# Scatters of the first phase spread over slots, two weight chunks kept on chip, ids moved behind the stream: a macaron block on one core

## The chip, the core and the metric

The kernel runs on one core of a Trainium2 chip. Its engines are TensorE (PE for matmuls, PEld for loading the stationary operand), VectorE (DVE), ScalarE (ACT), GpSimd (POOL) and SyncE (SP), which here issues most DMAs. The metric is the device time of one execution in microseconds, lower is better.

## The reference, cut to what matters

```
x = x + 0.5 * ffn(layernorm(x))
x = x + attention(layernorm(x))          # groups of 64 tokens, 16 heads of 16, causal
x = x + 0.5 * ffn(layernorm(x))

def ffn(x):                              # 4096 tokens, H = 256
    xn = rmsnorm(x)
    p, i = top_k(softmax(xn @ router_w.T), 2)       # 8 experts
    rw = p / sum(p)
    # each expert takes its first 640 tokens, in order
    xg = x[dispatch]
    eout = (silu(xg @ rg) * (xg @ ru)) @ rd         # 256 -> 1024 -> 256, one for each expert
    routed = scatter_add(eout * weight)
    shared = silu(x @ sg) * (x @ su) @ sd           # 256 -> 2048 -> 256
    return shared + routed
```

Both feed-forward networks have the same weights and the same input layout. Results are float32.

## The kernel before

**Numbers.** Each float32 operand of a matmul is split into two float16 parts, hi and lo (`split`, L102 to L107: ACT makes hi on L105, DVE makes lo on L106). A product is three matmuls: hi by hi, hi by lo, lo by hi (`TERMS`).

**Phases.** There are 4096 tokens, in 32 tiles of 128 rows or 8 blocks of 512. Phase a runs the shared network of the first FFN over blocks 0 to 3 (`shared`, L392 on, 16 chunks of 128 columns for each block). Phase b runs the eight experts of the first FFN (`experts`, L435 on, 8 chunks each). Phase c runs the shared network for the other four blocks and then that of the second FFN for blocks 0 to 6. Phase d runs the second FFN's experts and its last shared block.

**The main stream.** A chunk of `shared` is 12 matmuls of 128x512 on L349 (gate and up) and 12 of 128x256 on L373 (down), 3.9 us together. Between them ACT makes sl on L360 (L356 in phases c and d), DVE multiplies it with up on L362, ACT rounds it to hh on L364, DVE takes the rest hl on L365. The down product of a chunk is deferred by one chunk, so that PE has the next gate product to run meanwhile. PSUM holds three gate and up tiles.

**The side stream.** Beside the main stream, `Tiles` (L696) runs one generator for each tile: load, layernorm statistics (`stats`, L142 to L150, whose last step rstd is a power on POOL), z on DVE (L162), split into X (`two`, L166), transposing DMA, router logits. A tile starts every `GAP_A` = 2 slots in phase a. A slot is run by `drive` (L739) after every 2.5 yields of the main stream, some 3.26 us. In phase c the side stream is the attention with the layernorm of the second FFN.

**Routing.** After the fourth tile of a block, `route` finds each token's two experts and their rows; a chain of small operations on POOL (L243 to L264) makes the weights. `scatter` (L322 to L337) then writes a tile's rows, with four tag columns behind them, to the experts' lists in DRAM: four copies (L328) and two indirect DMAs (L330), all on POOL. The block's four scatters come in four slots after one another; they stand behind `self.anchor` where that is set, and phase a does not set it.

**Expert rows.** `expert_load` (L416 on) loads an expert's tags (L420, SP) and its rows by a transposing DMA (L422, SP), and makes ids and weights of the rows on DVE (L429 to L433). `experts` loads a chunk's three weight pieces re (L446 twice and L449, SP), splits them into wc and wd, and runs the chunk for 640 rows. Two such buffers of each are there. Expert 0's rows are loaded at the end of phase a (and of c), while the main stream of that phase is still running.

**Order.** Each engine runs its instructions in one order, fixed when the kernel is built, by a scheduler that knows priorities and estimated times. `behind(True, k)` (L198) puts what is inside it behind the main stream's latest sl: k = 0 is ACT's on L360, k = 1 DVE's on L362. SP, POOL and each engine wait in that order: an instruction that waits for data holds those behind it.

Of the kernel before, what the change touches and what calls it, by code (L numbers as in the profile page):

```python
# [8 lines left out]
F32 = mybir.dt.float32  # L9
F32R = mybir.dt.float32r  # L10
F16 = mybir.dt.float16
BF16 = mybir.dt.bfloat16
I32 = mybir.dt.int32
# [7 lines left out]
P = 128  # L21
H = 256
# [15 lines left out]
class Net:  # L38
# [100 lines left out]
                self.split(self.sdw[:, 0, c:c + 2], self.sdw[:, 1, c:c + 2], r2)  # L139
            yield  # L140

    def stats(self, x, mv, rstd):  # L142
        nc = self.nc
        st = self.sm.tile([P, 6], F32, name="st")
        nc.vector.bn_stats(out=st, in_=x)
        nc.vector.bn_aggr(out=mv, in_=st)
        ve = self.sm.tile([P, 1], F32, name="ve")
        nc.vector.tensor_scalar(
            out=ve, in0=mv[:, 1:2], scalar1=LN_EPS, scalar2=1.0 / UP ** 2, op0=ALU.add, op1=ALU.mult)
        nc.gpsimd.tensor_tensor(out=rstd, in0=ve, in1=self.mhalf[:, :1], op=ALU.pow)  # L150

    def normed(self, x, mv, rstd, pool=False):

# [80 lines left out]
            fb["L"] = self.sm.tile([P, 4, 2, E], F32, name="L")  # L234
        nc.scalar.copy(fb["L"][:, t], p)

    def route(self, R, b, fb):

        nc = self.nc
        sm = self.sm  # L240
# [58 lines left out]
        if b == NB - 1:  # L299
            self.limits(R)  # L300
            yield
        for t in range(4):
            with self.tc.issue_after(self.anchor.ins) if self.anchor else nullcontext():
                self.scatter(R, b, fb, t, di, w1, dl, ef)
            yield

    def limits(self, R):

# [107 lines left out]
    def expert_load(self, R, e, hold):  # L416
        nc = self.nc
        rows = R["xg"][e * CAP:(e + 1) * CAP]
        tag = self.sm.tile([P, 5, 4], F32, name="tag")
        nc.sync.dma_start(out=tag, in_=rows[:, H:XW].rearrange("(t p) f -> p t f", p=P))  # L420
        xt = hold["x"] = self.xe.tile([P, 4, CAP], F16, name="xe")
        nc.sync.dma_start_transpose(out=xt, in_=rows[:, 0:H].bitcast(F16))  # L422
        yield
        yield
        yield
        ids = hold["id"] = self.cst.tile([P, 5], I32, name=f"eid{R['key']}{e}")
        w = hold["w"] = self.cst.tile([P, 5], F32, name=f"ew{R['key']}{e}")
        tk = self.sm.tile([P, 5], I32, name="tkb")
        nc.vector.tensor_tensor(out=tk, in0=tag[:, :, 0].bitcast(I32), in1=R["bits"][:, e], op=ALU.bitwise_and)  # L429
        nc.vector.tensor_tensor(out=ids, in0=tk.bitcast(F32), in1=R["off"][:, e], op=ALU.add)  # L430
        nc.vector.scalar_tensor_tensor(
            out=w, in0=tag[:, :, 3], scalar=float(e), in1=tag[:, :, 1], op0=ALU.is_equal, op1=ALU.mult)
        nc.vector.tensor_tensor(out=w, in0=w, in1=tag[:, :, 2], op=ALU.add)  # L433

    def experts(self, R, rg, ru, rd, cur, also=iter(())):  # L435

        nc = self.nc
        for e in range(E):
            x, ids, wts = cur["x"], cur["id"], cur["w"]
            outs = [self.ps_out.tile([P, BT], F32, name="po", tag="po") for _ in range(3)]  # L440
            cur = {}
            nxt = self.expert_load(R, e + 1, cur) if e < E - 1 else iter(())
            for c in range(8):
                r = self.raw.tile([P, 2, 2, P], F32, name="re", tag="raw")
                for i, s in enumerate((rg, ru)):
                    nc.sync.dma_start(  # L446
                        out=r[:, i], in_=s[e, :, c * P:(c + 1) * P].rearrange("(k p) f -> p k f", p=P))
                r2 = self.raw.tile([P, H], F32, name="re2", tag="raw2")
                nc.sync.dma_start(out=r2, in_=rd[e, c * P:(c + 1) * P])  # L449
                wc = self.raw.tile([P, 2, 2, 2, P], F16, name="wc")  # L450
                self.split(wc[:, 0], wc[:, 1], r)
                wd = self.raw.tile([P, 2, H], F16, name="wd")
                self.split(wd[:, 0], wd[:, 1], r2)
                h = self.hbuf()
                for t0, n in SUBS:
                    hs = [a[:, t0:t0 + n] for a in h]
                    for _ in self.gate_up(wc, x[:, :, t0:t0 + n], hs):
                        pass

                def fin(e=e, c=c, h=h, wd=wd, outs=outs, ids=ids, wts=wts):  # L460
                    self.down(outs, 5, h, wd, c, 8)
                    if c < 7:
                        return
                    key = R["key"], e
                    for t in range(5):
                        eo = self.raw.tile([P, H], F32, name="eo", bufs=5)
                        o = outs[t // 2][:, (t % 2) * H:(t % 2 + 1) * H]
                        if t % 2:
                            nc.scalar.activation(eo, o, AF.Copy, scale=wts[:, t:t + 1])
                        else:  # L470
                            nc.vector.tensor_scalar_mul(eo, o, wts[:, t:t + 1])  # L471
                        i = nc.gpsimd.indirect_dma_start(  # L472
                            out=R["acc"][:, :], out_offset=bass.IndirectOffsetOnAxis(ap=ids[:, t:t + 1], axis=0),
                            in_=eo, in_offset=None, bounds_check=T - 1, oob_is_err=False, compute_op=ALU.add).ins
                        if 0 < t < 4:
                            self.tc.declare_no_dep(i, group=str(key), reason="an expert's tokens are distinct")
                        self.tc.add_to_no_dep_group(str(key), i)

                self.defer(fin)
                next(nxt, None)  # L480
                if e and c in (2, 4, 6):
                    next(also, None)
            for _ in nxt:
                pass
# [177 lines left out]

    def front_steps(self, y, t, new_fb, keep=None):
        fb = new_fb(t)
        self.stats(y, fb["mv"][:, t, :], fb["rstd"][:, t:t + 1])
        yield
        X = self.xs.tile([P, XW], F32, name="X")
        xp = X[:, 0:H].bitcast(F16)
# [27 lines left out]
class Tiles:  # L696


    def __init__(self, make, count, gap, held=None):
        self.make, self.count, self.gap = make, count, gap  # L700
        self.held = held
        self.slot = 0
        self.live = []
        self.nxt = 0

    def done(self):
        return self.nxt == self.count and not self.live

    def steps(self):

# [3 lines left out]
        for one in list(self.live):  # L714
            with self.held.behind(one[0] >= 4 * PEB, 0, 1) if self.held else nullcontext():
                r = next(one[1], "end")
            if r == "end":
                self.live.remove(one)
            elif r == "stall":
                return  # L720
            yield
        self.slot += 1

# [35 lines left out]
def macaron(ctx, tc, x, w_qkv, ln_w, w_proj, router_w, rg, ru, rd, sg, su, sd, out):  # L759
# [20 lines left out]

    def tail(R, h, b, t):
        if t == 3:
            yield from n.route(R, b, fbs[(h, b)])

    def tile1(j):
        b, t = divmod(j, 4)
# [4 lines left out]
            nc.sync.dma_start(out=R1["acc"][j * P:(j + 1) * P], in_=y)  # L791
        yield from n.front_steps(y, t, new_fb(1, b))
        yield from tail(R1, 1, b, t)
        if j == 31:
            yield from n.expert_load(R1, 0, first[0])

# [14 lines left out]
    with n.phase("a", BT, 2, 16):  # L811
# [4 lines left out]
        n.keep_going(20)  # L816
        n.load_router(router_w)
        n.keep_going(16)
        tiles = Tiles(tile1, 32, GAP_A, n)
        run_slots(tiles, ready(1, 0))  # L820
        next(weights)
        for b in range(NA):
# [5 lines left out]
        n.experts(R1, rg, ru, rd, first[0], n.attn_weights(w_qkv, w_proj))  # L828
    with n.phase("c", BT, 2, 6, SLC):
        n.attn_init(ln_w)  # L830
        tiles = Tiles(tile2, 32, GAP_C)
        for b in range(NA, NB):
            drive(all_shared((1, b), b, R1["acc"], R1["acc"], tanh=True), tiles, RATE_C)
        for b in range(NC):
# [48 lines left out]
```

## Time and profile before

| what | us |
|---|---|
| median of 3 runs | 1821.59 (1820.73 to 1824.99) |
| the profiled execution | 1819.05 |
| its span in the profile | 1817.3 |
| PE busy | 1780.0 |
| DVE busy | 1194.9 |
| ACT busy | 951.5 |
| POOL busy | 753.0 |
| mean granted clock of PE | 0.996 of full speed |

The span is the profiled execution less 1.75 us around it. Busy times are those of instructions that compute or move, so a PE busy for 1780.0 us has 37 us in which no matmul ran, and some of the busy time is matmuls at a lower granted clock. In a row of a timeline the bracket gives the idle time of that engine ahead of the instruction and the instruction that ended it. A list of waits gives the same idle time, summed by what waited for what: total us, number, longest.

### The profile page before, as it was taken

To read this page: it belongs to the slowest core of one execution; us is meant where nothing else is said; L and a number is where in the kernel's file an instruction comes from. 1 tells how busy PE (TensorE), PEld (TensorE's weight loads), DVE (VectorE), ACT (ScalarE), POOL (GpSimd) and SP (SyncE) were. 2 spreads that over 40 slices of the span, in tenths; PEclk is the share of its full clock that TensorE was granted. 3 is DMA by queue.
4 is the path that set the end of the run, shared out by engine and by line. 5 is a ranking of instruction groups with operands and counts; after the bars stand their busy time and mean duration, and the time that the engine had idled before them with its cause. 6 is when DMAs were issued, how large, how long until landed. Compare 5 with 4: busy or idle time off the path is not lost.

```text
span 1817.3 us, 37386 instructions
## 1 busy us (share of the span) xinstructions
PE 1780.0 (98%) x13652; PEld 1199.6 (66%) x13652; DVE 1194.9 (66%) x2909; ACT 951.5 (52%) x2057; POOL 753.0 (41%) x1072
## 2 busy tenths in 40 slices
PE   8999999999999999999999999999999999999998
PEld 5655657777777556665656666566655677777765
DVE  6756546666666567877787777777756566666643
ACT  4433325555555456666666666666323455555542
POOL 6576620222111335576767677776430011122210
PEclk9999999999999999999999999999999999999999
DMA  7333142555453255667666675756212144455420
GB/s 215 89 105 112 41 69 73 129 127 118 112 118 75 59 102 96 133 115 140 123 134 135 117 152 111 143 101 127 59 28 66 35 108 110 115 116 124 98 48 13
DMA packets 439481, 185.95 MB, mean 102 GB/s; under 512 B 302337, under 2 KB 436669, under 8 KB 439296
## 3 DMA queue, kind: packets, MB, share of 16 engines
q1 hardware_dynamic: 420816, 161.60, 40.6%
q0 software_dynamic: 17664, 21.17, 6.9%
q8 instruction: 107, 1.75, 0.4%
q10 hardware_dynamic: 816, 0.79, 0.1%
q14 instruction: 78, 0.64, 0.1%
HBM read 78.95 MB, written 42.21 MB: 67 GB/s over the span
## 4 chain that ended last, share of the span: by engine, by line
PE 67%; POOL 9%; DVE 9%; issue 6%; ACT 5%; DMA 3%; SPq 1%; POOLq 0%; DVEq 0%; ACTq 0%
PE pgu L349 43%; PE po L373 21%; POOL xg L330 3%; DVE hl L365 2%; DVE sl L357 1%; DVE sl L362 1%; POOL S L607 1%; DVE amx L606 1%; ACT V L611 1%; ACT sl L356 1%; POOL rstd L150 1%; POOL X L328 1%; DVE S L601 1%; POOL e L618 1%; PE pqk L660 1%
## 5 line engine op out<-in xcount | busy, mean ns | idle before, releaser
L349 PE MATMUL pgu<-xb,sgu 128*128 128x512 f16 x3072 | 737.8, 380 | 8.9 <-DVE sl L357 5.6
L364 ACT CAST hh<-sl 128x512 f16<-128x512 f32 (+2 forms) x512 | 272.9, 533 | 535.9 <-DVE sl L362 533.3
L349 PE MATMUL pgu<-xe,wc 128*128 128x384 f16 (+1 forms) x3072 | 497.0, 299 | 0.0
L349 PEld LDWEIGHTS <-sgu 128*128 128x128 f16 x3072 | 293.1, 98 | 283.2 <-issue 15.8
L362 DVE SCALAR_TENSOR_TENSOR sl<-pgu,sl 128x512 f32<-128x512 f32 (+2 forms) x512 | 300.8, 588 | 244.9 <-PE pgu L349 218.1
L365 DVE TENSOR_TENSOR hl<-sl,hh 128x512 f16<-128x512 f32 (+2 forms) x512 | 316.0, 618 | 148.5 <-ACT hh L364 147.4
L373 PEld LDWEIGHTS <-hh 128*128 128x128 f16 x3328 | 321.2, 98 | 108.5 <-ACT hh L364 4.3
L349 PEld LDWEIGHTS <-wc 128*128 128x128 f16 x3072 | 300.6, 98 | 91.9
L373 PE MATMUL po<-sdw,hh 128*128 128x256 f16 x2048 | 349.6, 272 | 4.3 <-DVE xr L406 2.1
L373 PE MATMUL po<-sdw,hl 128*128 128x256 f16 x1024 | 249.4, 273 | 13.9 <-DVE hl L365 11.3
L373 PE MATMUL po<-wd,hh 128*128 128x256 f16 x1280 | 221.3, 273 | 0.0
L472 POOL DMA_INDIRECT out_dram<-eo,eidscatter x40 | 64.5, 1612 | 344.5 <-DVE eo L471 309.7
L373 PEld LDWEIGHTS <-hl 128*128 128x128 f16 x1664 | 162.7, 98 | 56.4 <-DVE hl L365 22.7
L360 ACT ACTIVATE sl<-pgu 128x384 f32<-128x384 f32 (+1 forms) x336 | 158.8, 473 | 62.5 <-PE pgu L349 34.4
L472 POOL DMA_INDIRECT acc<-eo,eidscatter x40 | 65.5, 1638 | 294.4 <-DVE eo L471 260.5
L357 DVE SCALAR_TENSOR_TENSOR sl<-sl,pgu 128x512 f32<-128x512 f32 x176 | 120.0, 682 | 53.9 <-ACT sl L356 52.8
L330 POOL DMA_INDIRECT xg<-X,di x128 | 132.1, 1032 | 50.0 <-issue 27.8
L373 PE MATMUL po<-wd,hl 128*128 128x256 f16 x640 | 147.9, 273 | 0.0
L105 ACT ACTIVATE wc<-re 128x512 f16<-128x512 f32 x128 | 80.6, 630 | 79.6 <-PE pgu L349 63.0
L356 ACT ACTIVATE sl<-pgu 128x512 f32<-128x512 f32 x176 | 104.3, 592 | 28.2 <-PE pgu L349 26.6
L106 DVE SCALAR_TENSOR_TENSOR wc<-re,wc 128x512 f16<-128x512 f32 x128 | 88.3, 690 | 28.8 <-ACT wc L105 28.6
L607 POOL TENSOR_TENSOR S<-S,amx 128x1024 f32<-128x1024 f32 x32 | 63.6, 1989 | 70.9 <-DVE amx L606 70.5
(155 smaller groups left out, 1725.2 us busy)
## 6 DMA issues: line engine op xcount, KB each, us to landing
re<-in_L_ffn_rg_dram SPq DMA_DIRECT2D x128, 128.0 KB, 2.4
re<-in_L_ffn_ru_dram SPq DMA_DIRECT2D x128, 128.0 KB, 2.4
re<-in_L_ffn_rd_dram SPq DMA_DIRECT2D x128, 128.0 KB, 2.5
y<-acc SPq DMA_DIRECT2D x64, 128.0 KB, 2.2
y<-in_L_attn_x_dram SPq DMA_DIRECT2D x32, 128.0 KB, 2.1
acc<-xr SPq DMA_DIRECT2D x16, 256.0 KB, 2.4
out_dram<-xr SPq DMA_DIRECT2D x16, 256.0 KB, 2.8
x<-y SPq DMA_DIRECT2D x28, 128.0 KB, 3.0
```

The source lines that it names most:

```text
L106: nc.vector.scalar_tensor_tensor(out=lo, in0=src, scalar=WS, in1=hi, op0=ALU.mult, op1=ALU.subtract)
L330: i = nc.gpsimd.indirect_dma_start(out=R["xg"][:, :], out_offset=bass.IndirectOffsetOnAxis(ap=di[:, t, k:k + 1], axis=0), in_=X, in_offset ...
L349: nc.tensor.matmul(p, lhsT=wc[:, w, i, k, :], rhs=x[:, 2 * a + k, :], start=(j == 0), stop=(j == 5))
L356: nc.scalar.activation(s, p, AF.Tanh, scale=0.5 / XP)
L357: nc.vector.scalar_tensor_tensor(out=s, in0=s, scalar=1.0, in1=p, op0=ALU.add, op1=ALU.mult)
L360: self.latest[0] = nc.scalar.activation(s, p, AF.Silu, scale=1.0 / XP).ins
L362: self.latest[1] = nc.vector.scalar_tensor_tensor(out=s, in0=ps[1], scalar=1.0 / XP / (2.0 * XP if tanh else 1.0), in1=s, op0=ALU.mult, op ...
L364: nc.scalar.copy(h[0], s)
L365: nc.vector.tensor_tensor(out=h[1], in0=s, in1=h[0], op=ALU.subtract)
L373: nc.tensor.matmul(o, lhsT=h[a][:, t * P:(t + 1) * P], rhs=wd[:, w], start=(c == 0 and j == 0 and t % 2 == 0), stop=(c == nch - 1 and j == 2),
L472: i = nc.gpsimd.indirect_dma_start(out=R["acc"][:, :], out_offset=bass.IndirectOffsetOnAxis(ap=ids[:, t:t + 1], axis=0), in_=eo, in_offset ...
L607: self.anchor = nc.gpsimd.tensor_tensor(out=S, in0=S, in1=mx.unsqueeze(2).to_broadcast([P, 16, 64]), op=ALU.subtract)
```

## The change

1. In phase a, the scatters of a block no longer run in the routing's own slots. They go to a list `tiles.extra`, from which one tile's scatter (four copies, two DMAs) is issued every two slots, behind the latest rstd on POOL, which `stats` now records as the anchor. The last block still has one tile for each slot, and phase c (`apart` = 1) too.
2. `first_chunks` loads the weights of the first expert's first two chunks in phase a (three DMAs of 256 KB), splits them there, and keeps the results in the constants' pool for both passes over the experts. Both passes then load expert 0's weights from chunk 2 on.
3. The four operations that make an expert's ids and weights are put behind the main stream's latest sl on DVE.

In the order of SP's instructions, where the experts begin, before had tag, rows (expert 0), the weights of chunk 0, tag, rows (expert 1), the weights of chunk 1; the changed kernel has tag, rows, tag, rows, the weights of chunk 2, of chunk 3. Before had the tags of six further experts in a row some places later; they are now one for each expert.

```diff
@@ -139,7 +139,7 @@
                 self.split(self.sdw[:, 0, c:c + 2], self.sdw[:, 1, c:c + 2], r2)
             yield
 
-    def stats(self, x, mv, rstd):
+    def stats(self, x, mv, rstd, anchor=False):
         nc = self.nc
         st = self.sm.tile([P, 6], F32, name="st")
         nc.vector.bn_stats(out=st, in_=x)
@@ -147,7 +147,9 @@
         ve = self.sm.tile([P, 1], F32, name="ve")
         nc.vector.tensor_scalar(
             out=ve, in0=mv[:, 1:2], scalar1=LN_EPS, scalar2=1.0 / UP ** 2, op0=ALU.add, op1=ALU.mult)
-        nc.gpsimd.tensor_tensor(out=rstd, in0=ve, in1=self.mhalf[:, :1], op=ALU.pow)
+        i = nc.gpsimd.tensor_tensor(out=rstd, in0=ve, in1=self.mhalf[:, :1], op=ALU.pow)
+        if anchor:
+            self.anchor = i
 
     def normed(self, x, mv, rstd, pool=False):
 
@@ -234,7 +236,7 @@
             fb["L"] = self.sm.tile([P, 4, 2, E], F32, name="L")
         nc.scalar.copy(fb["L"][:, t], p)
 
-    def route(self, R, b, fb):
+    def route(self, R, b, fb, tiles):
 
         nc = self.nc
         sm = self.sm
@@ -299,10 +301,19 @@
         if b == NB - 1:
             self.limits(R)
             yield
+        last = self.scatters(R, b, fb, di, w1, dl, ef, 1 if b == NB - 1 else tiles.apart)
+        if b == NB - 1 or tiles.apart == 1:
+            yield from last
+        else:
+            tiles.extra.append(last)
+
+    def scatters(self, R, b, fb, di, w1, dl, ef, every):
+
         for t in range(4):
-            with self.tc.issue_after(self.anchor.ins) if self.anchor else nullcontext():
+            with self.tc.issue_after(self.anchor.ins):
                 self.scatter(R, b, fb, t, di, w1, dl, ef)
-            yield
+            for _ in range(every):
+                yield
 
     def limits(self, R):
 
@@ -426,11 +437,31 @@
         ids = hold["id"] = self.cst.tile([P, 5], I32, name=f"eid{R['key']}{e}")
         w = hold["w"] = self.cst.tile([P, 5], F32, name=f"ew{R['key']}{e}")
         tk = self.sm.tile([P, 5], I32, name="tkb")
-        nc.vector.tensor_tensor(out=tk, in0=tag[:, :, 0].bitcast(I32), in1=R["bits"][:, e], op=ALU.bitwise_and)
-        nc.vector.tensor_tensor(out=ids, in0=tk.bitcast(F32), in1=R["off"][:, e], op=ALU.add)
-        nc.vector.scalar_tensor_tensor(
-            out=w, in0=tag[:, :, 3], scalar=float(e), in1=tag[:, :, 1], op0=ALU.is_equal, op1=ALU.mult)
-        nc.vector.tensor_tensor(out=w, in0=w, in1=tag[:, :, 2], op=ALU.add)
+        with self.behind(True, 1):
+            nc.vector.tensor_tensor(out=tk, in0=tag[:, :, 0].bitcast(I32), in1=R["bits"][:, e], op=ALU.bitwise_and)
+            nc.vector.tensor_tensor(out=ids, in0=tk.bitcast(F32), in1=R["off"][:, e], op=ALU.add)
+            nc.vector.scalar_tensor_tensor(
+                out=w, in0=tag[:, :, 3], scalar=float(e), in1=tag[:, :, 1], op0=ALU.is_equal, op1=ALU.mult)
+            nc.vector.tensor_tensor(out=w, in0=w, in1=tag[:, :, 2], op=ALU.add)
+
+    def first_chunks(self, rg, ru, rd):
+
+        nc = self.nc
+        r = self.raw.tile([P, 2, 2, 2 * P], F32, name="rf", tag="raw", bufs=4)
+        for i, s in enumerate((rg, ru)):
+            nc.sync.dma_start(out=r[:, i], in_=s[0, :, 0:2 * P].rearrange("(k p) f -> p k f", p=P))
+        r2 = self.raw.tile([P, 2, H], F32, name="rf2", tag="raw2", bufs=4)
+        nc.sync.dma_start(out=r2, in_=rd[0, 0:2 * P].rearrange("(k p) f -> p k f", p=P))
+        yield
+        yield
+        self.chunks = []
+        for c in range(2):
+            wc = self.cst.tile([P, 2, 2, 2, P], F16, name=f"wc{c}")
+            self.split(wc[:, 0], wc[:, 1], r[:, :, :, c * P:(c + 1) * P])
+            wd = self.cst.tile([P, 2, H], F16, name=f"wd{c}")
+            self.split(wd[:, 0], wd[:, 1], r2[:, c])
+            self.chunks.append((wc, wd))
+            yield
 
     def experts(self, R, rg, ru, rd, cur, also=iter(())):
 
@@ -441,16 +472,19 @@
             cur = {}
             nxt = self.expert_load(R, e + 1, cur) if e < E - 1 else iter(())
             for c in range(8):
-                r = self.raw.tile([P, 2, 2, P], F32, name="re", tag="raw")
-                for i, s in enumerate((rg, ru)):
-                    nc.sync.dma_start(
-                        out=r[:, i], in_=s[e, :, c * P:(c + 1) * P].rearrange("(k p) f -> p k f", p=P))
-                r2 = self.raw.tile([P, H], F32, name="re2", tag="raw2")
-                nc.sync.dma_start(out=r2, in_=rd[e, c * P:(c + 1) * P])
-                wc = self.raw.tile([P, 2, 2, 2, P], F16, name="wc")
-                self.split(wc[:, 0], wc[:, 1], r)
-                wd = self.raw.tile([P, 2, H], F16, name="wd")
-                self.split(wd[:, 0], wd[:, 1], r2)
+                if e == 0 and c < 2:
+                    wc, wd = self.chunks[c]
+                else:
+                    r = self.raw.tile([P, 2, 2, P], F32, name="re", tag="raw")
+                    for i, s in enumerate((rg, ru)):
+                        nc.sync.dma_start(
+                            out=r[:, i], in_=s[e, :, c * P:(c + 1) * P].rearrange("(k p) f -> p k f", p=P))
+                    r2 = self.raw.tile([P, H], F32, name="re2", tag="raw2")
+                    nc.sync.dma_start(out=r2, in_=rd[e, c * P:(c + 1) * P])
+                    wc = self.raw.tile([P, 2, 2, 2, P], F16, name="wc")
+                    self.split(wc[:, 0], wc[:, 1], r)
+                    wd = self.raw.tile([P, 2, H], F16, name="wd")
+                    self.split(wd[:, 0], wd[:, 1], r2)
                 h = self.hbuf()
                 for t0, n in SUBS:
                     hs = [a[:, t0:t0 + n] for a in h]
@@ -662,7 +696,7 @@
 
     def front_steps(self, y, t, new_fb, keep=None):
         fb = new_fb(t)
-        self.stats(y, fb["mv"][:, t, :], fb["rstd"][:, t:t + 1])
+        self.stats(y, fb["mv"][:, t, :], fb["rstd"][:, t:t + 1], keep is None)
         yield
         X = self.xs.tile([P, XW], F32, name="X")
         xp = X[:, 0:H].bitcast(F16)
@@ -696,15 +730,17 @@
 class Tiles:
 
 
-    def __init__(self, make, count, gap, held=None):
+    def __init__(self, make, count, gap, apart, held=None):
         self.make, self.count, self.gap = make, count, gap
         self.held = held
         self.slot = 0
         self.live = []
+        self.apart = apart
+        self.extra = []
         self.nxt = 0
 
     def done(self):
-        return self.nxt == self.count and not self.live
+        return self.nxt == self.count and not self.live and not self.extra
 
     def steps(self):
 
@@ -718,6 +754,10 @@
                 self.live.remove(one)
             elif r == "stall":
                 return
+            yield
+        for g in list(self.extra):
+            if next(g, "end") == "end":
+                self.extra.remove(g)
             yield
         self.slot += 1
 
@@ -780,7 +820,7 @@
 
     def tail(R, h, b, t):
         if t == 3:
-            yield from n.route(R, b, fbs[(h, b)])
+            yield from n.route(R, b, fbs[(h, b)], tiles)
 
     def tile1(j):
         b, t = divmod(j, 4)
@@ -791,6 +831,8 @@
             nc.sync.dma_start(out=R1["acc"][j * P:(j + 1) * P], in_=y)
         yield from n.front_steps(y, t, new_fb(1, b))
         yield from tail(R1, 1, b, t)
+        if j == 28:
+            yield from n.first_chunks(rg, ru, rd)
         if j == 31:
             yield from n.expert_load(R1, 0, first[0])
 
@@ -816,7 +858,7 @@
         n.keep_going(20)
         n.load_router(router_w)
         n.keep_going(16)
-        tiles = Tiles(tile1, 32, GAP_A, n)
+        tiles = Tiles(tile1, 32, GAP_A, GAP_A, n)
         run_slots(tiles, ready(1, 0))
         next(weights)
         for b in range(NA):
@@ -828,7 +870,7 @@
         n.experts(R1, rg, ru, rd, first[0], n.attn_weights(w_qkv, w_proj))
     with n.phase("c", BT, 2, 6, SLC):
         n.attn_init(ln_w)
-        tiles = Tiles(tile2, 32, GAP_C)
+        tiles = Tiles(tile2, 32, GAP_C, 1)
         for b in range(NA, NB):
             drive(all_shared((1, b), b, R1["acc"], R1["acc"], tanh=True), tiles, RATE_C)
         for b in range(NC):
```

## The prediction

> **What bounds the kernel now.** I read the page's totals first, then the waits of PE, then the waits of all engines, then the timeline around the places that they point to.
>
> ```profile
> PE 1780.0 (98%) x13652; PEld 1199.6 (66%) x13652; DVE 1194.9 (66%) x2909; ACT 951.5 (52%) x2057; POOL 753.0 (41%) x1072
> ```
>
> PE is busy 1780.0 of 1817.3 us. The change leaves every matmul in place, so only PE's idle time, and matmuls that run slowly after an idle time, can be won. I measured that for each matmul as the step from its start to the next one's start, less the median step of its form. The excess is 46.6 us in the whole run, and it lies in clusters. Each 81.5 us block of the attention phase has about 2.9 us of it, which the change does not touch. Three places remain.
>
> PE's longest single waits point at them (total us, times, longest us):
>
> ```profile
> PE pgu L349 <- ACT sl L360: 2.4, 1, 2.4
> PE po L373 <- DVE ve L148: 2.2, 1, 2.2
> PE po L373 <- DVE xr L406: 2.1, 2, 1.7
> ```
>
> The waits of the other engines tell what lies behind them:
>
> ```profile
> DVE z L162 <- POOL rstd L150: 33.0, 14, 5.1
> ...
> ACT wc L105 <- DMA re<-in_L_ffn_ru_dram: 16.6, 4, 6.3
> ...
> DVE tkb L429 <- DMA tag<-xg: 10.2, 11, 2.8
> ```
>
> *Place 1, phase a.* The timeline (start, duration, engine and line, idle time before with its releaser) at 137 us:
>
> ```profile
> 136.92 0.97 POOL L330 DMA_INDIRECT xg<-X,di  x1 [0.30 <-issue]
> ...
> 138.04 0.58 POOL L150 TENSOR_TENSOR rstd<-ve,mhalf 128x1 f32<-128x1 f32 x1
> ...
> 138.66 0.41 DVE L162 TENSOR_SCALAR z<-y,mv,rstd 128x256 f32<-128x256 f32 x1 [5.06 <-POOL rstd L150]
> ...
> 139.08 0.66 DVE L365 TENSOR_TENSOR hl<-sl,hh 128x512 f16<-128x512 f32 x1
> ...
> 139.79 0.28 PE L373 MATMUL po<-sdw,hl 128*128 128x256 f16 x1 [2.24 <-DVE ve L148]
> ```
>
> POOL issues a block's eight scatters back to back from 127.83 to 137.89. The next rstd stands behind them, z waits 5.06 us for it, hl stands behind z on DVE, and PE waits 2.24 us. The name ve in PE's row is only the semaphore that came last; hl ended at 139.74. PE's excess is 2.40 us here and 1.63 us more at 141 to 144, where the stretch 140 to 145 has a granted clock of 0.66. Two more bursts cost 1.38 us (at 42.0, z idle 4.04) and 0.70 us (at 168.0, z idle 4.65). Together 6.11 us.
>
> *Place 2, the way from phase a to the first experts:*
>
> ```profile
> 248.08 4.61 SPq L422 DMA_TRANSPOSE xe<-xg  x1
> ...
> 252.92 0.40 SPq L446 DMA_DIRECT2D re<-in_L_ffn_rg_dram  x1
> 253.37 0.46 SPq L446 DMA_DIRECT2D re<-in_L_ffn_ru_dram  x1
> ...
> 254.86 3.06 SPq L422 DMA_TRANSPOSE xe<-xg  x1
> ...
> 256.20 0.63 ACT L105 ACTIVATE wc<-re 128x512 f16<-128x512 f32 x1 [6.28 <-DMA re<-in_L_ffn_ru_dram]
> 256.74 0.58 ACT L360 ACTIVATE sl<-pgu 128x512 f32<-128x512 f32 x1
> ...
> 257.37 3.90 PE L349 MATMUL pgu<-xb,sgu 128*128 128x512 f16 x10 [2.38 <-ACT sl L360]
> ```
>
> The transposing load of expert 0's rows holds SP for 4.61 us. The first weight chunk is issued after it, ACT's split of that chunk waits 6.28 us, and the main stream's sl stands behind that split. PE idles 2.38 us, and ten matmuls then take 3.90 us in place of 2.32. Excess 4.12 us.
>
> *Place 3, the same way from phase c to phase d*, around 1363 to 1378: ACT's wc waits 5.66 and 3.28 us for weights, DVE's tkb (ids) waits for tags, and PE's last wait there is 1.74 us for xr. Excess 1.36, 1.34 and 1.90, together 4.60 us, with no lower clock.
>
> All that the change can reach is 6.11 + 4.12 + 4.60 = 14.8 us.
>
> **The change, part by part.**
>
> *Scatters.* POOL's work keeps its size. A pair of scatters is 2 x 1.28 us by the start-to-start of the rows, and with four copies at about 0.13 us it is 3.1 us. The order of the changed kernel puts one pair behind each rstd, where there were four pairs behind one. Per block POOL has 8 x 1.28 = 10.2, 16 copies 2.1, four rstd at 0.55 = 2.2 and the routing chain about 6.5 us (three powers at 1.04 to 1.49, the rest 0.20 to 0.53), 21 to 22 of the 26 us that a block of tiles takes. A tile comes every 6.5 us, so a pair that starts behind one rstd is over some 3 us before the next is wanted. What cover has a late z? The three stalls tell: 4.04 - 1.38 and 5.06 - 2.40 both give 2.66 us, 4.65 - 0.70 gives 3.95. A z that waits up to 2.66 us costs PE nothing. One pair is 2.6 us, and a pair with a power of the chain behind it 3.6, so some new loss is possible. Bounds: nothing to 2.5 us; I take 0.3, nearest to the cover. Gain 6.1 - 0.3 = **+5.8 us**.
>
> *First chunks.* Six DMAs for each of two expert passes go (12 of 128 KB), with 8 ACT and 8 DVE splits. Three DMAs of twice the size come around 45 to 50 us, with 4 ACT and 4 DVE splits between the stream's operations. In 120 to 140 us ACT is busy 5.70 of 20 us and DVE 9.19, so 4 x (0.63 or 0.41) on ACT and 4 x (0.69 or 0.42) on DVE lie beside PE; without that cover they would cost at most their sum, 4.3 us. I take nothing. SP has six fewer issues at each boundary.
>
> But SP's order changes: the first weight load is now chunk 2, and it stands behind both transposing loads, which before had chunk 0 between them. At place 2: 248.08 + 4.61 = 252.69; tag 0.43 with gaps, so the second transpose starts about 253.4; with 3.06 us it ends at 256.4; rg goes at 256.5, ru at 257.1. From ru's issue to wc was 2.83 and 2.75 us for the first two chunks, so the split of chunk 2 starts at 259.85. Now ACT's order: sl of chunk 59 stands ahead of that split, so the 2.38 us wait goes, but hh of chunk 59 stands behind it. It starts at 260.4 and ends at 261.0. PE has the next twelve gate and up matmuls to run ahead and is through at 257.3, so it waits until 261.06, that is 3.75 us, and loses about 1.6 more to the half clock, as it did after 2.38 us. Loss 5.35 us against 4.12: -1.2. If the second transpose takes 4.61 us like the first, the wait is 5.3 us and the loss 6.9: -2.8. If the weights were there in time it would be +4.1. I take **-1.5**, near to the 3.06 us row.
>
> *Ids behind the stream's sl.* The four DVE operations (0.15 to 0.17 us) of an expert now stand behind a chunk's sl, one expert at a time, and the tag loads are spread likewise; six to eight experts' came in a bunch before. Behind them on DVE stand hl and the next sl, delayed by 0.5 us, and nobody needs the ids before the expert's last chunk. At place 3 this takes the 1.90 us wait with xr away. There the first weight load comes behind both transposes as well: 1356.67 + 2.77, tag, 2.99, rg 1363.3, ru 1363.9, wc with 2.71 us at 1366.6. DVE's half of the split is through at 1367.9, and the sl behind it at 1368.5. PE, without the earlier 1.36, is through with what it has at 1366.26 and waits 2.3 us. If that costs the clock as in place 2, 1.6 more: 3.9 against 4.60, **+0.7**; bounds -0.5 (4.61 us transpose) and +4.6.
>
> The one unknown in this is the clock. Gaps of 2.24 and 2.38 us were followed by half clock, 1.74 and 1.90 were not; 2.3 lies on the side of the drop. [...]
>
> The rest (experts, attention, the tail) keeps its order on PE and POOL: nothing.
>
> **Sum.** 5.8 - 1.5 + 0.7 = 5.0 us off the profiled execution of 1819.05 us, that is 1814.05. That execution is 2.54 us below the median of the runs, 1821.59. On the median I forecast **1816.6 us**.
>
> **The rivals.**
>
> *Clock kept at place 3.* The 2.3 us wait is too short for the drop: 1.6 us better, **1815.0**. For it: 1.90 us was. Against: 2.24 was not.
>
> *The boundary stalls go.* If the second transpose lets SP go sooner, or chunk 2's split is not ahead of what the stream needs, places 2 and 3 bring 4.1 and 4.6: 14.5 us, **1807.1**. For it: the two chunks whose splits stood in the stalls are gone. Against: both transposes' rows hold SP for 3 us, and ACT's order has the split ahead of hh.
>
> *Given back.* The second transpose takes the first one's time at both places (-2.8 and -0.5), and phase a keeps 1.5 us of its loss: 4.6 - 3.3 = 1.3, **1820.3**.
>
> *Slower: POOL falls behind in phase a.* POOL runs at 85% and a pair now stands ahead of every later rstd and of the routing powers. Where pair, copies and a chain power meet ahead of an rstd, z waits 2.6 + 0.5 + 1.1 = 4.2 us, 1.5 over the cover of 2.66. The same place then holds the last block's scatters back, and with them tag, both transposes and the first weights. Once it costs more than 5.3 us in the seven blocks (0.76 a block) the change loses; at 1.7 a block it costs 11.9 in place of 0.3: 5.0 - 11.6 = -6.6, **1828.2**. Against: POOL idles 4.80 us ahead of the last block's dl and 3.85 ahead of its first scatter.
>
> **How the numbers follow.** Chances: forecast 0.40, clock kept 0.12, stalls go 0.16, given back 0.21, slower 0.11. A measurement of this kernel can tell about 0.3% from no change, 5.5 us, so faster is below 1816.1 and the forecast lies at this border. Faster: 0.16 + 0.11 + 0.4 of the forecast's 0.40 = 0.43. Slower: 0.08 (the case's upper part, above 1827.1). The rest, 0.49, is the same. The range leaves out most of the slower case and the best half of the stalls that go: 1809.0 to 1822.5.
>
> **What would show it.** In the changed profile: DVE z's waits for rstd fall from 5.1 us at the longest to below 2.7, and PE has no wait above 1 us between 30 and 240 us; at the first boundary PE's wait for sl is gone, and one of 3 to 5 us for hh stands some 3 us later, with a lower clock behind it, while the second L422 row follows the first and the first L446 row comes after both; at the second boundary one PE wait of about 2.3 us behind L362, and no wait of tkb above 1 us. A PE wait of 1 us at each block in phase a, a boundary with no PE wait, or scatters of the last block after 247 us would prove me wrong.

## The result and the profile after

The changed kernel takes 1810.76 us (median of 6 runs, 1809.20 to 1811.83), the kernel before 1822.24 (6 runs). The ratio is 0.9933, 95% interval 0.9920 to 0.9946: 11.5 us faster by the medians, where 5.0 was forecast and 1816.6 was the number. In a second comparison the ratio is 0.9945 (0.9932 to 0.9959), 9.5 us by the medians.

The profiled execution of the changed kernel took 1811.83 us, its span is 1809.8, 7.5 less than before's. PE's line and three rows of PE's waits (total us, times, longest), to be held against those of before:

```profile
PE 1777.4 (98%) x13652; PEld 1200.8 (66%) x13652; DVE 1194.7 (66%) x2905; ACT 949.8 (52%) x2053; POOL 752.2 (42%) x1072
```

```profile
PE pgu L360 <- DVE sl L373: 2.9, 3, 1.7
PE po L384 <- ACT hh L375: 2.2, 3, 1.7
PE pgu L360 <- issue: 1.5, 2, 1.2
```

The waits of 2.4, 2.2 and 1.7 us for sl on L360, ve and xr are gone. At the boundaries one of 1.7 us for hh is left (the first) and one of 1.7 us for sl (the second; L373 is the old L362). The 1.2 us put down to "issue" (no releaser in the profile) lies near 1290 us, of which more below. The wait of z for rstd, the mark of phase a, was 33.0 us in total and 5.1 at the longest, and is now:

```profile
DVE z L164 <- POOL rstd L150: 4.3, 9, 0.8
```

At the first boundary the timeline of the changed kernel has both transposing loads, then the weights of chunk 2, then ACT's split of them, and PE behind it:

```profile
240.64 2.86 SPq L433 DMA_TRANSPOSE xe<-xg  x1
...
244.18 3.12 SPq L433 DMA_TRANSPOSE xe<-xg  x1
247.54 0.38 SPq L480 DMA_DIRECT2D re<-in_L_ffn_rg_dram  x1
247.97 0.46 SPq L480 DMA_DIRECT2D re<-in_L_ffn_ru_dram  x1
...
251.08 0.63 ACT L105 ACTIVATE wc<-re 128x512 f16<-128x512 f32 x1 [6.65 <-DMA re<-in_L_ffn_rg_dram]
251.62 0.60 ACT L375 CAST hh<-sl 128x512 f16<-128x512 f32 x1
...
252.28 0.39 PE L384 MATMUL po<-sdw,hh 128*128 128x256 f16 x2 [1.66 <-ACT hh L375]
```

The order is the one that the prediction worked out; the first transposing load held SP for 2.86 us and not 4.61, 1.75 us less, and PE's wait is 1.66 us and not 3.75.

The measure of the prediction, the excess of a step between matmuls over the median step of its form, summed over a stretch, gives the account of all runs. Phase a is here all of the 225 us that follow the main stream's first matmul, small excesses included. The first 4 us of them, long before the first scatter at 29.8 us, have up to 1.1 us of excess of their own: 1.11 in before and 0.43 in the changed kernel, 0.91 and 0.85 when both are repeated.

| kernel (profiled execution) | phase a | 1st boundary | 2nd boundary | ratio to before |
|---|---|---|---|---|
| before | 8.07 | 4.13 | 4.63 | 1 |
| before, again | 9.32 | 3.26 | 4.28 | |
| changed | 0.25 | 2.70 | 2.45 | 0.9933 |
| changed, again | 0.68 | 4.74 | 2.89 | 0.9945 |
| scatters alone | 0.23 | 3.00 | 4.92 | 0.9955 |
| chunks alone | 7.83 | 4.71 | 3.13 | 0.9998 |
| ids alone | 7.42 | 3.18 | 2.12 | 0.9983 |
| scatters + chunks | 0.38 | 4.57 | 3.10 | 0.9958 |
| scatters + ids | 0.14 | 3.05 | 2.04 | 0.9938 |
| chunks + ids | 8.60 | 5.30 | 1.96 | 0.9987 |
| changed, expert 1's rows later | -0.10 | 4.02 | 1.56 | 0.9943 |
| changed, splits held back | 0.31 | 0.01 | -0.01 | 0.9920 |
| both of these | 0.33 | 0.00 | -0.01 | 0.9906 |
| changed, scatters in fours | 1.58 | 5.63 | 2.68 | 0.9960 |

For the first pair the three stretches give 7.8 + 1.4 + 2.2 = 11.4 us. Of the 7.8, 0.7 lies in the first 4 us and has nothing to do with the scatters; 7.1 remain. The spans differ by 7.5 only, because the changed kernel's execution has 4.3 us of excess at 1286 to 1294 that before's has not; the repeated profiles (below) show that the kernel before has such a place too.

### The profile page after: what moved, and what is told of

It reads as the page before. It is cut to its first block, busy times and chain, and to the rows that moved or that the text cites. A ratio compares the mean times of both kernels' runs of the same rounds, so it can differ in the third digit from the quotient of the medians.

```text
span 1809.8 us, 37358 instructions
## 1 busy us (share of the span) xinstructions
PE 1777.4 (98%) x13652; PEld 1200.8 (66%) x13652; DVE 1194.7 (66%) x2905; ACT 949.8 (52%) x2053; POOL 752.2 (42%) x1072
## 3 DMA queue, kind: packets, MB, share of 16 engines
q8 instruction: 107, 1.75, 0.4%
## 4 chain that ended last, share of the span: by engine, by line
PE 65%; DVE 9%; issue 9%; POOL 8%; ACT 5%; DMA 2%; SPq 1%; POOLq 0%; DVEq 0%; ACTq 0%
PE pgu L360 42%; PE po L384 21%; POOL xg L341 2%; DVE sl L368 2%; DVE hl L376 2%; POOL S L641 1%; DVE amx L640 1%; DVE S L635 1%; DVE sl L373 1%; ACT sl L367 1%; POOL e L652 1%; ACT V L645 1%; POOL X L339 1%; POOL ss L592 1%; DMA y<-acc 1%
## 5 line engine op out<-in xcount | busy, mean ns | idle before, releaser
L360 PE MATMUL pgu<-xb,sgu 128*128 128x512 f16 x3072 | 736.1, 379 | 10.3 <-DVE sl L368 5.6
L360 PE MATMUL pgu<-xe,wc 128*128 128x384 f16 (+1 forms) x3072 | 497.6, 299 | 0.0
L360 PEld LDWEIGHTS <-sgu 128*128 128x128 f16 x3072 | 292.8, 98 | 282.8 <-issue 15.2
L373 DVE SCALAR_TENSOR_TENSOR sl<-pgu,sl 128x512 f32<-128x512 f32 (+2 forms) x512 | 301.1, 588 | 265.0 <-PE pgu L360 230.8
L360 PEld LDWEIGHTS <-wc 128*128 128x128 f16 x3072 | 300.6, 98 | 91.8
```

Source lines behind the costliest of these rows:

```text
L360: nc.tensor.matmul(p, lhsT=wc[:, w, i, k, :], rhs=x[:, 2 * a + k, :], start=(j == 0), stop=(j == 5))
L373: self.latest[1] = nc.vector.scalar_tensor_tensor(out=s, in0=ps[1], scalar=1.0 / XP / (2.0 * XP if tanh else 1.0), in1=s, op0=ALU.mult, op ...
```

## The experiments

The ratios above have intervals of about 0.0009 to 0.0017 on either side. The excess of a profile is the finer measure, but it is that of one execution. Ratios of different rows were mostly not measured beside each other; *both of these*, *chunks + ids* and the changed kernel, again, were.

**Scatters alone.** The other two parts are undone:

```diff
-                if e == 0 and c < 2:
+                if False:
-        if j == 28:
-            yield from n.first_chunks(rg, ru, rd)
-        with self.behind(True, 1):
+        with nullcontext():
             nc.vector.tensor_tensor(out=tk, ...
```

> Only the scatters are spread as in the changed kernel; chunks and ids as before. Theory (the stalls of phase a are what the burst of eight scatters costs, 6.1 us in the profile of before): 6 to 8 us faster than before, about 1815; no wait of z for rstd above 2.7 us, no excess above 0.6 us between 30 and 240 us; the first boundary keeps its 4.1 us and the second its 4.6. Rival (most of the gain comes from the boundaries): 3 us faster or less.

Measured: 0.9955 (0.9939 to 0.9972), 8 us faster. Phase a's excess falls to 0.23 us, the second boundary keeps 4.92. The theory holds: this part alone makes between two thirds and four fifths of the gain. The first boundary's 3.00 is less than 4.1, since the half clock did not follow its wait of 1.82 us here: ten matmuls behind it took 2.47 us, where before has 3.90 behind 2.38.

**Chunks alone.** Scatters go back into the routing's slots (`yield from` with `every` = 1, no anchor in `stats`), ids are not put behind the stream.

> Only the two chunks are kept on chip; scatters and ids as before. Theory: the first boundary goes from 4.1 to about 2.7 us of excess, the second from 4.6 to about 4; phase a keeps its three stalls; 1.5 to 2.5 us faster, about 1820. Rival from the prediction (first weights behind both transposes, and half clock behind the longer wait): the first boundary costs 5.4 us or more, no faster than before. Second rival (the kept chunks take all of the boundary away): 8 us faster.

Measured: 0.9998 (0.9989 to 1.0008). My theory for this run falls: the first boundary costs 4.71 us, more than before, and what the second gains (3.13 us) is lost there. It is no gain, as the first rival has it, but not by the prediction's mechanism. PE does not wait for hh behind ACT's split, but for hl, which stands on DVE behind expert 1's weights of the rows, and these wait for their tag:

```profile
256.01 0.17 DVE L439 SCALAR_TENSOR_TENSOR ewscatter<-tag 128x5 f32<-128x5 f32 x1 [6.67 <-DMA tag<-xg]
...
257.04 0.34 PE L380 MATMUL po<-sdw,hl 128*128 128x256 f16 x1 [2.87 <-DVE hl L372]
```

**Ids alone.**

> Only the ids are put behind the stream's sl; scatters and chunks as before. Theory: the wait of PE for xr at the second boundary (1.9 us of excess) goes, nothing else: 1 to 2 us faster, about 1820.5. Rival (the ids were hidden anyway, the next wait takes their place): within 0.5 us of before.

Measured: 0.9983 (0.9974 to 0.9993), 3 us faster, somewhat more than the theory's 1 to 2 (the interval reaches down to 1.3). The second boundary falls from 4.63 and 4.28 us to 2.12, by 2.2 to 2.5, where the wait for xr alone was 1.9.

**Scatters and chunks, without the ids.**

> The changed kernel without its third part: scatters spread and two chunks kept, ids in a bunch. Theory (parts add up): 1.5 to 2 us slower than the changed kernel, about 1812.5, with the whole of it at the second boundary. Rival (the ids' place also sets the first boundary, where six tag loads stood in a row on SP): 3 us or more slower than the changed kernel, with a first boundary above 3.5 us of excess.

Measured: 0.9958 (0.9941 to 0.9974), about what the scatters give alone, and 4.57 us at the first boundary. The rival is right that the ids' place decides what PE waits for at the first boundary. It is not shown to decide how much: the changed kernel has 2.70 us there in one execution and 4.74 in another. The timeline of this run:

```profile
240.12 4.81 SPq L433 DMA_TRANSPOSE xe<-xg  x1
244.99 0.58 SPq L431 DMA_DIRECT2D tag<-xg  x1
...
247.94 0.17 DVE L443 SCALAR_TENSOR_TENSOR ewscatter<-tag 128x5 f32<-128x5 f32 x1 [6.64 <-DMA tag<-xg]
...
248.23 0.68 DVE L376 TENSOR_TENSOR hl<-sl,hh 128x512 f16<-128x512 f32 x1
248.97 0.39 PE L384 MATMUL po<-sdw,hl 128*128 128x256 f16 x1 [2.84 <-DVE hl L376]
```

With two chunks' loads gone, expert 1's tag is the next load behind the first transposing one. DVE's weights of its rows wait 6.64 us for it, the stream's hl stands behind them, and PE waits 2.84 us. So without the ids' move the kept chunks only swap a wait on ACT for one on DVE, as in the run with the chunks alone. The six tags in a row, which the rival named, have no part in it; it is one tag.

**Scatters and ids, without the chunks.**

> The changed kernel without the kept chunks: scatters spread, ids behind the stream's sl. Theory (the kept chunks bring nothing of their own once the ids are out of the way: the profile with the ids alone has 3.1 and 1.6 us at the two boundaries, the changed kernel 2.7 and 2.4): within 1.5 us of the changed kernel, a ratio to before of about 0.9935. Rival (chunks and ids only work together): 3 us or more slower than the changed kernel.

Measured: 0.9938 (0.9922 to 0.9955). Its excess is 0.14, 3.05 and 2.04, that of the changed kernel 0.25 to 0.68, 2.70 to 4.74 and 2.45 to 2.89. The kept chunks bring nothing that these runs can show. The theory holds.

**Expert 1's rows later.** The first weight loads go ahead of the second transposing load:

```diff
-                next(nxt, None)
+                if e or c > 2:
+                    next(nxt, None)
```

> The changed kernel, but expert 1's tag and rows are loaded after the weights of chunks 2 and 3, so that the first weight load stands behind one transposing load. Theory of the prediction (the second transposing load is what the first split waits for): both boundaries' waits shrink by some 2 us each, 3 to 4 us faster than the changed kernel. Rival (the scheduler puts the split as much earlier into ACT's order as the weights come earlier, so it holds sl in place of hh): within 1 us of the changed kernel, PE's wait at the first boundary is for sl again.

Measured: 0.9943 (0.9926 to 0.9959), as the changed kernel. Counted from the main stream's first matmul, the split starts 2.3 and 3.4 us earlier than in the changed kernel's two profiles, and the order on ACT is made anew around it. From the timeline, and from the table of windows (us; then PE, PEld, DVE, ACT, POOL busy, granted clock, DMA share, GB/s):

```profile
247.53 0.63 ACT L105 ACTIVATE wc<-re 128x512 f16<-128x512 f32 x1 [6.73 <-DMA re<-in_L_ffn_ru_dram]
...
248.69 1.46 PE L360 MATMUL pgu<-xb,sgu 128*128 128x512 f16 x6 [2.84 <-ACT sl L371]
```

```profile
246.00:249.00 3.00, 0.31 (x2) 0.18 (x2) 0.71 (x2) 1.43 (x4) 0.00 (x0) 1.00 0.84 222
249.00:252.00 3.00, 2.15 (x11) 0.88 (x10) 2.40 (x5) 1.95 (x4) 0.00 (x0) 1.00 1.13 242
```

The split still waits 6.73 us, now with sl behind it, as in the kernel before. The rival is right: the arrival of the weights is not what counts at the first boundary. (At the second, 1.56 is somewhat less than 2.45.)

**Splits held back.** Loads stay; the splits of expert 0's chunks 2 and 3 stand behind the sl of expert 0's chunk 0:

```diff
+                    with self.behind(e == 0 and c < 4, 2, 3):
                     wc = self.raw.tile([P, 2, 2, 2, P], F16, name="wc")
                     self.split(wc[:, 0], wc[:, 1], r)
...
+                if e == 0 and c == 0:
+                    self.latest = self.latest[:2] * 2
                 self.defer(fin)
```

> The changed kernel, but the splits of expert 0's chunks 2 and 3 stand behind the sl of expert 0's chunk 0 on ACT and DVE; loads stay where they are. Theory (what costs PE is not when the weights come but that the split of early weights stands ahead of the stream's own operations): excess below 0.8 us at each boundary, 3.5 to 4.5 us faster than the changed kernel, ratio to before about 0.991. Rival (the wait only moves to the gate product of chunk 2): within 1 us of the changed kernel, with a PE wait of 2 us or more for wc a chunk later.

Measured: 0.9920 (0.9903 to 0.9936). Both boundaries are at nothing, 0.01 and -0.01 us, and no wait comes in their place:

```profile
245.00:250.00 5.00, 5.00 (x35) 3.14 (x33) 2.05 (x3) 1.94 (x4) 0.00 (x0) 1.00 1.07 207
250.00:255.00 5.00, 5.00 (x33) 3.00 (x31) 1.41 (x3) 1.49 (x3) 0.00 (x0) 1.00 0.54 161
255.00:260.00 5.00, 5.00 (x31) 2.83 (x29) 2.08 (x7) 1.21 (x2) 0.00 (x0) 1.00 0.07 2
```

PE is busy for all of 245 to 260, while the first weight load is issued at 248.29, where the changed kernel's two profiles have 247.54 and 248.55. The theory holds for the waits, and no wait for wc a chunk later, the rival's, is there. By the ratios this version is 2 to 5 us faster than the changed kernel, which was not measured beside it. By its code it rests on the two kept chunks, which PE works on while the splits are held back; holding back was not tried without them.

**Both of these**, measured beside the changed kernel.

> The changed kernel with the splits of expert 0's chunks 2 and 3 behind expert 0's first sl, and the first weight loads ahead of expert 1's rows as well. Theory (the place of the split on ACT is all that mattered): as with the splits held back alone, 4 to 5.5 us faster than the changed kernel in the same call, no excess above 0.6 us at either boundary. Rival (the order of SP's loads still matters): 1.5 us or more away from the kernel with the splits held back alone.

Measured: 1804.80 us, 0.9906 (0.9891 to 0.9922), against 1812.20 and 0.9945 for the changed kernel: 7.4 us faster, more than the 4 to 5.5 expected. The changed kernel's boundaries cost 4.74 + 2.89 us in its profile there, which fits. This version beats both kernels. The order of SP's loads no longer matters: the excess is that of the splits held back alone.

**Scatters in fours.** Two tiles' scatters are issued together every four slots:

```diff
+            if every > 1 and t % 2 == 0:
+                continue
-            for _ in range(every):
+            for _ in range(every if every == 1 else 2 * every):
                 yield
```

> The changed kernel, but in phase a two tiles' scatters are issued together every four slots (four DMAs in a row, 5.1 us, where the changed kernel has two and before had eight). Theory of the cover (a z that waits up to 2.7 us costs PE nothing): waits of z of up to 2.5 to 3 us behind the four, excess in phase a 0 to 2 us, 0 to 2 us slower than the changed kernel. Rival (any burst longer than a pair is paid in full): 4 us slower or more, with a stall in most of the seven blocks.

Measured: 0.9960 (0.9946 to 0.9974), 3 to 5 us slower than the changed kernel by the ratios, where 0 to 2 was expected. In phase a the longest z wait is 3.52 us and the excess 1.58, 1.16 of it right behind that wait:

```profile
64.45 0.41 DVE L164 TENSOR_SCALAR z<-y,mv,rstd 128x256 f32<-128x256 f32 x1 [3.52 <-POOL rstd L150]
...
66.72 1.46 PE L362 MATMUL pgu<-xb,sgu 128*128 128x512 f16 x6 [1.02 <-DVE sl L375]
```

3.52 less the cover of 2.66 is 0.9, and PE waits 1.02 us. So the cover that the prediction read from the bursts of eight is near the mark for this wait, and the rival (a stall in most blocks) falls: no other place of phase a has an excess above 0.3 us. The first boundary costs 5.63 us, 0.9 to 2.9 more than in the changed kernel: the wait for hh is 3.44 us there, with a granted clock of 0.66 behind it (255 to 260 us). Its first transposing load took 4.38 us. Whether the fours cause that was not tried.

**Chunks and ids, without the scatters.**

> Second and third part without the first: chunks kept and ids behind the stream's sl, scatters in a burst. Theory (kept chunks alone gain nothing because the tag of expert 1, now right behind the first transposing load, comes late for the ids, which hold hl; with the ids out of the way the wait that remains is shorter): 4 to 6 us faster than before, with phase a's 6.1 us left. Rival (ids and chunks do not depend on each other): 3 us faster, the sum of the two alone.

Measured: 0.9987 (0.9978 to 0.9996), 2 us faster, nearer to the rival's 3 us than to the 4 to 6 expected. The second boundary is at 1.96, the first at 5.30: with the ids out of the way the wait for hh that the prediction described is there in full (3.10 of the 5.30 us). My theory for this run falls: it took for granted that the wait that remains is short.

**Both kernels once more.**

> The kernel before, profiled once more. Theory (its stalls are set by its order, the same in every execution): the same clusters as in its first profile, 6.1 us in phase a, 4.1 and 4.6 at the boundaries, within 1 us each. Rival (a part of them, the half clock after a wait above all, is chance): one of the clusters differs by 1.5 us or more.

> The changed kernel once more, beside the others of this call. Theory: 11 to 13 us faster than before; its profile has the boundaries at 2.7 and 2.4 us again, and not the 4.3 us at 1286 to 1294 of its first profile, which was a hiccup of that execution. Rival (the 4.3 us belong to the changed kernel): they are there again.

Measured: before again has 9.32, 3.26 and 4.28 us. The wait of 2.24 us in phase a is there as in the first profile, but no half clock behind it. The first row of windows is the first profile's, the second the repeat's:

```profile
140.00:145.00 5.00, 5.00 (x25) 2.35 (x24) 3.84 (x22) 1.76 (x6) 2.28 (x9) 0.66 0.40 107
140.00:145.00 5.00, 3.81 (x26) 2.14 (x27) 4.96 (x26) 2.77 (x8) 1.50 (x7) 1.00 0.39 107
```

So the rival holds: the places come from the order, but a part of their cost is chance. The changed kernel again is 0.9945, 9.5 us faster where 11 to 13 was expected; the boundaries are not those of its first profile, and a pause near 1290 us is there again. Its first boundary has the longer form of the wait:

```profile
252.88 0.83 PE L384 MATMUL po<-sdw,hh 128*128 128x256 f16 x4 [2.82 <-ACT hh L375]
```

```profile
253.00:256.00 3.00, 3.00 (x12) 1.38 (x11) 2.31 (x6) 1.57 (x4) 0.00 (x0) 0.52 0.65 190
```

So the first boundary's excess in one kernel differs by 2 us between two executions. The excess near 1290 is 2.59 us here and 2.66 us in before (1297 to 1301). It does not belong to the change.

## Why the prediction was right or wrong

**Scatters: the mechanism right, the size too small.** Forecast 5.8 us, found 7.1 and 8.6 in the two pairs, the first 4 us of the stream left out. The error is in the size of the stalls, not in what replaces them: behind those 4 us the changed kernel has no excess, where 0.3 was forecast. I added the three largest clusters, 6.11, and left out three small ones that the change removes too, 0.36 at 38.4 us, 0.37 at 115.7 and 0.20 at 200.7; the stretch behind the first 4 us has 6.96 in the same trace. In the repeated profile of before the stalls at 41 and 168 us are larger (1.75 and 1.64), there is a new one of 1.0 near 110, and the half clock is missing (1.00 granted from 140 to 145 us, where the first profile has 0.66).

**Chunks: the wait right, its cause half seen.** Forecast -1.5 at the first boundary, found +1.4 and -1.5. The wait for hh behind the split is there. Its length goes with the time that the two transposing loads and the tag between them hold SP: 6.56, 7.60, 7.70 and 7.97 us together in the four profiles where PE waits for hh (changed, changed again, chunks + ids, scatters in fours), and waits of 1.66, 2.82, 3.10 and 3.44 us. The prediction's 4.61 + 0.43 + 3.06 = 8.10 us with a wait of 3.75 lies close to the same line, so the working was right and its first term, taken from one row, was not what the changed kernel got (2.86 and 3.02). The half clock that the sum charged behind this wait came in the repeat (0.52 granted from 253 to 256 us) and not in the first profile (1.00 from 250 to 260 us); that the repeat has the forecast -1.5 is in part luck. But the account gave the swap to the chunks alone. By the runs, chunks alone swap ACT's wait for DVE's wait for a tag, and only with the ids moved does hh become the last.

**Ids: right at the second boundary, missed at the first.** Forecast +0.7 with the half clock, found 2.2 and 1.4. The wait behind the old L362 is there (1.73 and 2.2 us against 2.3), but the clock held (1.00 granted from 1363 to 1368 us in both profiles), which was the rival *clock kept*: the 1.6 us for the half clock were charged on a reading that does not hold (below). That the ids also decide what PE waits for at the first boundary was missing: without their move it is a tag on DVE. What their move is worth there is not shown: with the chunks kept, the first boundary has 4.71 and 4.57 us without it and 2.70, 4.74 and 5.30 with it.

**The sum.** 7.1 + 1.4 + 2.2 = 10.7 and 8.6 - 1.5 + 1.4 = 8.5 us in the two pairs; 5.0 was forecast. Half of the difference is at the first boundary in the first pair (2.9 us) and most of it in the scatters in the second (2.8). The measured 1810.76 us lies near the fast end of the range, and nearer to the 1807.1 of *the boundary stalls go* than to the forecast, although these stalls did not go: no term was too large, and two or three were too small.

**The rivals.** *The boundary stalls go* was ruled out for the right reason: the split stands ahead of hh. The held-back splits show that this order was the whole of it. *Given back* and *POOL falls behind* did not come; as before, POOL idles 3.86 us ahead of the last block's first scatter (3.85 before):

```profile
229.01 1.11 POOL L341 DMA_INDIRECT xg<-X,di  x1 [3.86 <-ACT sl L371]
```

## What to carry to other kernels

Where a steady stream shares an engine with work that waits for a load, as ACT here with a split that waited 6.28 us in before and 6.65 us in the changed kernel, look at what stands behind the waiting instruction: moving the split behind the stream's operations removed both boundary stalls here (0.01 and -0.01 us of excess left), and bringing the load forward (4.02 and 1.56) or saving it (4.71 and 3.13), without that, did not. When a stall is to be valued, sum the excess over the whole stretch that has its cause, not only its largest clusters. Parts of a change should be tried alone and in pairs: the kept chunks alone only swapped one wait for another, and which wait came last depended on another part.

## What was not expected of the hardware

**The half clock after a wait is partly chance.** Behind the wait of 2.24 us in phase a, before had a granted clock of 0.66 from 140 to 145 us, which cost 1.63 us of excess (0.34 x 5 is 1.7). Behind the same wait, before, again, had 1.00 (the rows above). A wait of the same length at the second boundary of the changed kernel, again, was not followed by it either (granted clock 1.00 from 1363 to 1368 us):

```profile
1364.22 1.46 PE L360 MATMUL pgu<-xb,sgu 128*128 128x512 f16 x6 [2.25 <-DVE sl L373]
```

Waits of 1.66 to 2.01 us at the boundaries were not followed by it: the granted clock was 1.00 behind 1.66 and 1.73 us in the changed kernel (250 to 260 and 1363 to 1368 us) and behind 1.74 us in before (1375 to 1382 us), and ten matmuls of 128x512 took 2.47 us behind 1.82 us (scatters alone) and 2.39 behind 2.01 (ids alone). Of six waits from 2.38 to 3.44 us there five were:

| kernel | wait, us | behind it |
|---|---|---|
| before | 2.38 | ten matmuls of 128x512 in 3.90 us; 0.72 granted from 255 to 260 us |
| changed, again | 2.82 | 0.52 granted from 253 to 256 us |
| scatters + chunks | 2.84 | two matmuls of 128x256 in 0.63 us, 0.38 later on |
| chunks alone | 2.87 | two matmuls of 128x256 in 0.63 us |
| changed, scatters in fours | 3.44 | 0.66 granted from 255 to 260 us |

One was not, the 2.84 us wait with expert 1's rows later, whose windows above stay at 1.00. The prediction read its numbers as an edge between 1.90 and 2.24 us (its 1.74 and 1.90 are the idle time and the excess of one wait, that for xr). That reading falls.

What decides between the two is not shown by these runs.

**The first transposing load of the first boundary held SP for 2.86 to 4.81 us**, though its shape is the same in every kernel: 4.61 in before, 2.86 and 3.02 in the changed kernel, 4.81 in scatters + chunks. With the tag and the second load behind it, it goes with the length of the wait for hh there (figures above). What makes it long stays open.

**PE and DVE paused near 1290 us** in five profiles where before takes some 1822 us beside them, both kernels among them (before's first profile lacks it), and in none of the eight where it takes 1817. In the five the gate and up matmuls have 0.6 to 1.6 us of waits put down to "issue", in the eight none are listed. PE stops several times for 0.2 to 1.2 us with no releaser in the profile, while POOL finishes a block's scatters. In before, again, the row of DVE is:

```profile
1299.68 0.21 DVE L632 RECIPROCAL rc<-py 128x8 f32<-128x8 f32 x1 [4.11 <-remote]
```

Its cause was not looked for; it added 2.6 us of excess to an execution, and 4.3 to the changed kernel's first, with 0.56 granted behind it (1291 to 1294 us).
